# Second stage of a four-layer graph network: another layout of the score rows in DRAM, read back in two pieces, and a copy instead of an addition

## The chip, the cores and the metric

The kernel runs on one core of one Trainium2 chip. The metric is the device time of one execution in microseconds (us); lower is better. A core has a matrix engine (PE), a vector engine (DVE), an activation engine (ACT), a general engine (POOL), a sequencer that here issues the DMAs (SP), and 16 DMA engines that they all share. Each engine works through its own queue in order.

## The reference

Four graph layers run one after the other on x, 128 batches of 128 nodes with 128 features, with one adjacency matrix for each batch. Each layer takes the layer norm of x with relu, computes its update, and adds it to x. The change lies in the second layer, whose score between nodes i and j comes from the absolute difference of their features:

```python
D = jnp.abs(x[:, :, None, :] - x[:, None, :, :])
h = jnp.einsum('bijc,oc->bijo', D, W1) + b1
m = jnp.mean(h, axis=(0, 1, 2))
v = jnp.mean((h - m) ** 2, axis=(0, 1, 2))
h = (h - m) / jnp.sqrt(v + EPS) * g1 + be1
h = _leaky(h)
s = jnp.einsum('bijo,uo->biju', h, W2)[..., 0] + b2[0]
s = jnp.where(A_init > 0, s, NEG)
A = jax.nn.softmax(s, axis=-1)
y = jnp.einsum('bij,bjc->bic', A, x)
```

After that y goes through a linear map, a second batch norm and a third linear map. The scores are symmetric: s(i, j) = s(j, i). Because m and v are taken over all batches, no score can be formed before h is known for all of them.

## The kernel before

The program has three stages. The **first stage** computes layer one, and for layer two the linear values hp of every pair of nodes together with their mean and variance. Thanks to the symmetry only the pairs (i, i + k mod 128) with k from 0 to 64 are needed. The values go out to DRAM as tiles HP, 2 MB for a batch[...].

The **second stage** is `two_stages` from line 770 on. It fetches the values again (`fetch`, L662: two reads of 1 MB for a batch into tiles z, into a ring of 10 buffers), normalises and activates them on ACT and DVE (L850, L854, L868), and PE turns them into scores (`products`, L825). The order of the instructions is written out by hand: `slot(b)` is one step of a software pipeline and handles one batch at each of its places, and `at(slot, place, work)` hangs extra work on a place of a slot: "am", "e", "p", "a", "l", "s" in order of the slot. `slot` copies the scores of the batch before to SBUF (su, L846), PE puts them in order of k (`by_k`, L832), and DVE writes them to a tile sk (`to_sk`, L839 and L841): for each of the 128 nodes i and each of the G = 4 batches of a group, a row of 65 scores, k = 0 to 64, with the first and last halved.

What the softmax needs is a square: node i in a partition, node j along the row. The row of i has to be moved to the right by i places, another distance in each partition[...]. So `chain(turn)`, which handles one group of four batches, sends the rows through DRAM:

- `to_rows` (L902), at place "s" of slot 4 x turn + 5: one DMA writes the 65 scores of row i to DRAM, starting at place i of a row that is ROW = 192 long (128 + 64). Row i starts at 192 i, its scores at 193 i; that is the step `ROW + 1`. The other places were set to zero once (`no_scores`, L579) and stay zero. The DMA right behind it (L905) loads the group's x.
- `from_rows` (L909), two slots later: one DMA reads the four squares of 128 x 192 back into a tile u. It can be issued only when the write has landed, and SP waits for that.
- `folded` (L920), at place "l" of slot s0 = 4 x turn + 9, on DVE: columns 128 to 191 of u are added to columns 0 to 63. These are the scores that had run over the end of the row.
- `turned("put", ...)` (L894) at place "p" of the next slot: PE transposes u, which by symmetry gives the other half of the square. `scores` (L924, L925) on DVE adds the two and masks with `cap`.
- The softmax and the products with the features follow in the next slots, and at slot s0 + 7 the results go out (L957, L958): x1 as x, and y.

There are two DRAM buffers `slots` that take turns, and two buffers of u. POOL has two operations for a group in this stage: x1 = x + bt (L916) and cap (L914), in `normed` at place "e" of slot s0. Between slots 12 and 38 the stage has extra work of `brief`, mostly on DVE (L1045), which prepares and decides for stage three. `final` marks the last group.

The **third stage** computes layers three and four; the change doesn't touch it.

Of the kernel before, what the change touches and what calls it, by code (L numbers as in the profile page):

```python
# [9 lines left out]
F32 = mybir.dt.float32  # L10
# [4 lines left out]
OP = mybir.AluOpType  # L15
AX = mybir.AxisListType

P = 128
G = 4
# [7 lines left out]

KH = 32
KC = 8
ROW = P + 2 * KH  # L30
ON_POOL = {1, 3}
BY_MAX = 0
FETCHED = 10
# [136 lines left out]
def tile_gnn_stack(ctx: ExitStack, tc: tile.TileContext, a: dict, out: bass.AP):  # L170
    nc = tc.nc
# [48 lines left out]

    slots = [dr.tile([G, P, ROW], F32, tag=f"rows{n}", name=f"rows{n}") for n in range(2)]
    AGG = [dr.tile([P, G, P], F32, tag=f"a{g}", name=f"a{g}") for g in range(NG)]
# [44 lines left out]
    def two_stages(general):  # L267
# [6 lines left out]
        with tc.tile_pool(name="c0", bufs=1) as c0, tc.tile_pool(name="p0", bufs=2) as p0:  # L274
# [278 lines left out]
            found = {}  # L553
            zero = c0.tile([P, ROW], F32, name="zero")
            nc.gpsimd.memset(zero, 0.0)
# [21 lines left out]
            def no_scores():  # L577
                for r in slots:
                    nc.sync.dma_start(r.rearrange("g i r -> i g r"), zero[:, None, :].to_broadcast([P, G, ROW]))  # L579

# [191 lines left out]
        with tc.tile_pool(name="c1", bufs=1, reuse_waits="tile") as c1, \  # L772
# [28 lines left out]
            for n in range(2):  # L801
                t = c1.tile([P, G, 1 + 2 * KH], F32, name=f"sk{n}")
# [76 lines left out]
            def chain(turn):  # L879

                rows, own_sk = slots[turn % 2], sk[turn % 2]
                t = {}
                g = (turn - 1) % NG
                final = turn == NG - 1
# [15 lines left out]
                def to_rows():  # L900
                    to = rows[0, 0, 0:1]
                    nc.sync.dma_start(bass.AP(tensor=to.tensor, offset=to.offset,  # L902
                                              ap=[[ROW + 1, P], [P * ROW, G], [1, 1 + 2 * KH]]), own_sk)
                    t["x"] = p1.tile([P, G, P], F32, name="x", bufs=3)
                    nc.sync.dma_start(t["x"], X[g])  # L905

                def from_rows():
                    t["u"] = p1.tile([P, G, ROW], F32, name="u")
                    nc.sync.dma_start(t["u"], rows.rearrange("g i r -> i g r"))  # L909

                def normed():
                    t["h"] = pre_norm(p1, t["x"], MV1[:, g], RS1[:, g])
# [3 lines left out]
                    nc.gpsimd.tensor_tensor(t["x1"], t["x"], over_group(bt), OP.add)  # L916

                def folded():
                    u = t["u"]
                    nc.vector.tensor_tensor(u[:, :, 0:2 * KH], u[:, :, 0:2 * KH], u[:, :, P:], OP.add)  # L920

                def scores():
                    t["e"] = p1.tile([P, G, P], F32, name="e1")
# [30 lines left out]
                def stored():  # L954
                    nc.vector.bn_stats(ST2[:, g, :], t["y"].rearrange("p a b -> p (a b)"))
                    if g not in Y:
                        nc.sync.dma_start(X[g], t["x1"])  # L957
                        nc.sync.dma_start(Z[g], t["y"])  # L958

                at(G * turn + G + 1 - final, "s", to_rows)  # L960
                at(G * turn + G + 3 - 2 * final, "s", from_rows)
                at(s0, "e", normed)
                at(s0, "p", lambda: turned("pt", t["h"]))
                at(s0, "l", folded)
                at(s0 + 1, "am", lambda: copied("hT", "pt"))
                at(s0 + 1, "p", lambda: turned("put", t["u"]))
# [667 lines left out]
```

## Time and profile before

| | us |
|---|---|
| median of 3 runs | 2674.77 (2673.55 to 2675.49) |
| profiled execution, device time | 2676.09 |
| profiled execution, span from first to last instruction | 2674.2 |

Busy shares of the span: PE 91%, DVE 92%, ACT 89%, POOL 64%. They are averages over three stages with different limits. In the second stage, about 1450 to 2245 us, POOL is nearly idle (0 to 1 tenths in the slices) while DVE and PE are busy at 8 to 9 tenths. DMAs of this stage:

| DMA | count | KB each | median us from issue to landing |
|---|---|---|---|
| z <- hp (L662) | 248 | 1024 | 13.7 |
| rows <- sk (L902) | 32 | 130 | 13.0 |
| u <- rows (L909) | 32 | 384 | 11.4 |
| x <- x, all uses | 118 | 256 | 4.8 |
| z <- y (L958) | 27 | 256 | 11.8 |

The profile page shows the span in 40 equal slices of 66.9 us, with the DMA rate in the last row. In a timeline each row has the start, the duration, the engine, the line of the code, the operation, out<-in, the count and in brackets the idle time of the engine just before and what ended it. In a table of waits each row has who waited for whom, us in total, times, and the longest.

### The profile page before, as it was taken

Reading aid. Unit: us, or ns where it says so; the run is one execution under the profiler, and the core shown is the slowest. Engines: PE = TensorE matmul, PEld = TensorE weight load, DVE = VectorE, ACT = ScalarE, POOL = GpSimd, SP = SyncE. Lnnn points to the kernel's source line nnn. Section 1 sums busy time; section 2 is a strip of 40 time slices with the busy share of each in tenths; the row PEclk is TensorE's granted clock in tenths of the full one; section 3 lists DMA queues with packets and bytes.
Section 4 is the critical chain, followed back from the end, with each engine's and each line's share of the span. In section 5 each row is a group of like instructions: output and inputs, shape, how many; then the busy total and the mean of one; then the engine's idle time right before and its main releaser. Section 6 shows DMA issues by size and latency. Waiting matters only on the chain.

```text
span 2674.2 us, 41925 instructions
## 1 busy us (share of the span) xinstructions
PE 2437.0 (91%) x14521; PEld 1162.1 (43%) x14521; DVE 2469.6 (92%) x4738; ACT 2380.3 (89%) x2821; POOL 1706.1 (64%) x1628
## 2 busy tenths in 40 slices
PE   6999999999999999999997988888888886999997
PEld 3333333333333333333332443444444445777776
DVE  5999999999999999999998789988888886899997
ACT  5999999999999999999998877788778874999997
POOL 6999999999999999999985000010101123666663
PEclk8999999999999999999998999999999998999999
DMA  3555555555555555555542999999999992021211
GB/s 101 201 206 209 212 212 211 212 213 205 209 205 209 205 210 204 217 204 216 205 197 93 409 409 384 392 409 410 411 410 411 410 373 81 21 68 56 64 37 34
DMA packets 185426, 611.43 MB, mean 229 GB/s; under 512 B 31987, under 2 KB 99702, under 8 KB 121718
## 3 DMA queue, kind: packets, MB, share of 16 engines
q1 hardware_dynamic: 184768, 608.50, 59.1%
q8 instruction: 118, 1.93, 0.3%
q14 instruction: 102, 0.84, 0.1%
q10 hardware_dynamic: 438, 0.17, 0.0%
HBM read 312.58 MB, written 296.03 MB: 228 GB/s over the span
## 4 chain that ended last, share of the span: by engine, by line
PE 37%; ACT 24%; DVE 15%; DMA 12%; POOL 7%; issue 4%; SPq 0%; POOLq 0%; DVEq 0%; ACTq 0%
PE hp L338 16%; ACT d L376 9%; ACT z L352 7%; DMA z<-hp 4%; PE hp L341 4%; DMA rows<-sk 4%; PE ps L825 4%; POOL d L328 4%; DMA u<-rows 3%; DVE z L868 3%; ACT o L473 2%; PE pk L832 2%; ACT hn L473 2%; PE xp L414 1%; DVE e L1502 1%
## 5 line engine op out<-in xcount | busy, mean ns | idle before, releaser
L328 POOL TENSOR_TENSOR d<-xe 128x2048 f32<-128x2048 f32 x256 | 1073.8, 4205 | 36.4 <-PE hp L338 34.5
L338 PE MATMUL hp<-d,w1T 128*64 128x512 f32 x4096 | 994.1, 601 | 57.6 <-ACT z L352 54.5
L376 ACT ACTIVATE d<-d 128x2048 f32<-128x2048 f32 x384 | 733.8, 1924 | 19.8 <-POOL d L328 19.5
L328 DVE TENSOR_TENSOR d<-xe,xp 128x2048 f32<-128x2048 f32 x256 | 583.6, 2280 | 7.0 <-POOL xe L423 4.0
L352 ACT COPY z<-hp 128x1024 f32<-128x1024 f32 x512 | 519.1, 1015 | 9.7 <-PE hp L338 4.5
L338 PEld LDWEIGHTS hp<-d,w1T 128*64 128x64 f32 x4096 | 276.9, 136 | 559.5 <-issue 455.3
L916 POOL TENSOR_TENSOR x<-x,bt 128x512 f32<-128x512 f32 x32 | 48.8, 1525 | 665.7 <-DMA x<-x 494.1
L366 DVE BATCH_NORM_STATS2 st<-z 128x6 f32<-128x512 f32 x512 | 354.7, 693 | 6.2 <-ACT z L352 6.1
L367 DVE BATCH_NORM_STATS2 st<-z 128x6 f32<-128x512 f32 (+1 forms) x512 | 336.4, 657 | 0.0
L868 DVE SCALAR_TENSOR_TENSOR z<-z 128x2048 f32<-128x2048 f32 x128 | 299.5, 2340 | 5.5 <-ACT z L850 5.3
L850 ACT ACTIVATE z<-z,bias,scale 128x2048 f32<-128x2048 f32 x128 | 267.5, 2090 | 8.9 <-DVE bias L762 7.7
L854 ACT ACTIVATE zr<-z,bias,scale 128x2048 f32<-128x2048 f32 x128 | 267.7, 2092 | 0.5 <-DMA z<-hp 0.5
L341 PE MATMUL hp<-both_t,xw 128*64 128x512 f32 x1024 | 265.2, 592 | 0.0
L825 PE MATMUL ps<-z,w2z 128*32 128x512 f32 x1024 | 140.9, 622 | 61.2 <-DVE z L868 60.5
L832 PEld LDWEIGHTS pk<-pick,su 128*128 128x128 f32 x1024 | 126.8, 195 | 147.8 <-DVE su L846 112.9
L832 PE MATMUL pk<-pick,su 128*128 128x16 f32 x1024 | 139.4, 268 | 34.6 <-DVE su L846 33.8
L825 PE MATMUL ps<-zr,w2r 128*32 128x512 f32 x1024 | 142.5, 629 | 0.0
L341 PEld LDWEIGHTS hp<-both_t,xw 128*64 128x64 f32 x1024 | 77.6, 137 | 142.2 <-issue 142.2
L825 PE MATMUL ps<-z,w2l 128*32 128x512 f32 x1024 | 138.4, 610 | 0.0
L1525 PE MATMUL pv<-wr,e 128*128 128x128 f32 x1024 | 134.0, 278 | 2.1 <-ACT wr L1450 1.1
L1525 PEld LDWEIGHTS pv<-wr,e 128*128 128x128 f32 x1024 | 124.1, 192 | 8.4 <-ACT wr L1450 1.8
L1409 ACT ACTIVATE h<-x,nb,rs 128x128 f32<-128x128 f32 x256 | 106.0, 491 | 20.1 <-POOL nb L1404 18.4
(241 smaller groups left out, 3808.3 us busy)
## 6 DMA issues: line engine op xcount, KB each, us to landing
hp<-z SPq DMA_DIRECT2D x248, 1024.0 KB, 4.0
z<-hp SPq DMA_DIRECT2D x248, 1024.0 KB, 13.7
x<-x SPq DMA_DIRECT2D x118, 256.0 KB, 4.8
u<-rows SPq DMA_DIRECT2D x32, 384.0 KB, 11.4
x<-in_x_dram SPq DMA_DIRECT2D x32, 256.0 KB, 5.6
adj<-in_adj_dram SPq DMA_DIRECT2D x32, 256.0 KB, 5.9
out_dram<-x SPq DMA_DIRECT2D x32, 256.0 KB, 2.4
z<-y SPq DMA_DIRECT2D x27, 256.0 KB, 11.8
```

The lines of the kernel that those rows point to most:

```text
L328: eng.tensor_tensor(d, ahead, x[:, None, None, :].to_broadcast([P, 2, KC, P]), OP.max if t == BY_MAX else OP.subtract)
L338: nc.tensor.matmul(hp[64 * hh:64 * hh + 64, c:c + 512], w1T2 if by_max else w1T, d[:, hh, c:c + 512], start=True, stop=not by_max, skip_gr ...
L341: nc.tensor.matmul(hp[64 * hh:64 * hh + 64, c:c + 512], XW[i // NT // 2][:, i // NT % 2, :], both_t.rearrange("p h k i -> p h (k i)")[:, h ...
L352: nc.scalar.copy(half_of(b, t), linear.pop(i))
L366: nc.vector.bn_stats(st[:, 2 * t, :], hs[:, 0:512])
L367: nc.vector.bn_stats(st[:, 2 * t + 1, :], hs[:, 512:1024 - P * last])
L376: nc.scalar.activation(diffs[i], diffs[i], AF.Abs)
L825: nc.tensor.matmul(ps[32 * c:32 * c + 32, :], w[:, w0:w0 + 32], v[:, 512 * c:512 * c + 512], start=j0 == 0, stop=w is w2r, skip_group_chec ...
L832: nc.tensor.matmul(pk[:, kk, 0:16], su[:, kk, :], pick.rearrange("p h j -> p (h j)"), start=True, stop=True)
L850: nc.scalar.activation(z0, z0, AF.Identity, bias=bias1, scale=scale1[:, 0:1])
L854: nc.scalar.activation(zr, z1, AF.Relu, bias=bias1, scale=scale1[:, 0:1])
L868: nc.vector.scalar_tensor_tensor(z0, z0, 0.01, z0, op0=OP.mult, op1=OP.max)
```

## The change

The rows in DRAM become 129 long, and the scores of row i are written straight, from the start of row i (step `ROW`). Read back with a step of 128 and not 129, row i begins i places earlier relative to its scores, so they appear moved to the right by i: an element at 128 i + c is place c - i of row i. This works while the 65 scores end before column 128, that is for i up to 63. The nodes from 64 on are read with their own start, 64 columns further on: into columns 64 to 191 of u. So `from_rows` has two DMAs, each for 64 partitions and 128 columns. Places that were never written are zero, as before.

In the upper half of u the columns 128 to 191 hold what had run over the end, and columns 0 to 63 hold nothing, so `folded` is a copy there and nothing at all in the lower half: 64 partitions, 4 x 64 elements. It runs on POOL, except in the last group, where it stays on DVE.

```diff
-ROW = P + 2 * KH
+ROW = P + 1
...
                 def to_rows():
                     to = rows[0, 0, 0:1]
                     nc.sync.dma_start(bass.AP(tensor=to.tensor, offset=to.offset,
-                                              ap=[[ROW + 1, P], [P * ROW, G], [1, 1 + 2 * KH]]), own_sk)
+                                              ap=[[ROW, P], [P * ROW, G], [1, 1 + 2 * KH]]), own_sk)
...
                 def from_rows():
-                    t["u"] = p1.tile([P, G, ROW], F32, name="u")
-                    nc.sync.dma_start(t["u"], rows.rearrange("g i r -> i g r"))
+                    t["u"] = p1.tile([P, G, P + 2 * KH], F32, name="u")
+                    for half in range(2):
+                        i = slice(P // 2 * half, P // 2 * half + P // 2)
+                        of = rows[0, 0, 0:1]
+                        of = bass.AP(tensor=of.tensor, offset=of.offset + (P + 1) * P // 2 * half,
+                                     ap=[[P, P // 2], [P * ROW, G], [1, P]])
+                        nc.sync.dma_start(t["u"][i, :, P // 2 * half:P // 2 * half + P], of)
...
                 def folded():
-                    u = t["u"]
-                    nc.vector.tensor_tensor(u[:, :, 0:2 * KH], u[:, :, 0:2 * KH], u[:, :, P:], OP.add)
+                    u = t["u"][P // 2:]
+                    eng = nc.vector if final else nc.gpsimd
+                    eng.tensor_copy(u[:, :, 0:2 * KH], u[:, :, P:])
```

Here P is 128, KH 32 and G 4. The tile of zeros that fills the DRAM rows at the start is [P, ROW] and shrinks with ROW.

## The prediction

> **What bounds the kernel now.** I read the page's 40 slices first. The change touches only the second stage, which is the part in which the DMA engines are full.
>
> ```profile
> DMA  3555555555555555555542999999999992021211
> GB/s 101 201 206 209 212 212 211 212 213 205 209 205 209 205 210 204 217 204 216 205 197 93 409 409 384 392 409 410 411 410 411 410 373 81 21 68 56 64 37 34
> ```
>
> A slice is 66.9 us. From 1471 us (slice 23) the core moves about 410 GB/s for eleven slices, and the figure hardly changes. To see whether that is a ceiling or just what the engines ask for, I cut the stage into stretches (columns: length, busy us and instructions of PE, PEld, DVE, ACT, POOL, PE clock, DMA share, GB/s).
>
> ```profile
> 1480.00:1492.00 12.00, 11.88 (x104) 4.95 (x100) 9.98 (x14) 12.00 (x7) 0.00 (x0) 1.00 1.02 421
> 1648.00:1660.00 12.00, 10.61 (x73) 4.71 (x73) 11.86 (x20) 7.88 (x6) 0.00 (x0) 0.86 1.00 379
> 1804.00:1816.00 12.00, 11.58 (x90) 5.85 (x88) 9.47 (x14) 10.60 (x9) 0.50 (x1) 1.00 1.03 408
> 1710.12:1849.10 138.98, 123.73 (x966) 59.93 (x966) 123.12 (x188) 114.96 (x80) 18.72 (x12) 1.00 1.02 408
> 1934.14:2172.13 237.99, 206.52 (x1580) 99.36 (x1580) 201.91 (x311) 188.41 (x131) 33.87 (x20) 0.99 1.03 410
> ```
>
> Between 1582 and 1710 us DVE has the extra work of `brief` and the DMA rate falls below 380. Everywhere else it is 408 to 410, whether the engines run fast (1710 to 1849) or stall (1934 to 2172). I read that as a ceiling for this mix of transfers; 421 is the highest seen. Next the DMA issues of one late group (four batches) on SP.
>
> ```profile
> 1920.81 0.37 SPq L902 DMA_DIRECT2D rows<-sk  x1
> 1921.91 0.32 SPq L905 DMA_DIRECT2D x<-x  x1
> 1922.60 7.68 SPq L662 DMA_DIRECT2D z<-hp  x4
> 1934.14 0.37 SPq L909 DMA_DIRECT2D u<-rows  x1
> 1934.56 0.50 SPq L957 DMA_DIRECT2D x<-x  x1
> 1935.11 0.42 SPq L958 DMA_DIRECT2D z<-y  x1
> 1935.64 6.82 SPq L662 DMA_DIRECT2D z<-hp  x4
> ...
> 2172.13 0.37 SPq L909 DMA_DIRECT2D u<-rows  x1
> ```
>
> The u reads at 1934.14 and 2172.13 are ten groups apart, so one group takes 23.80 us. By the sizes in the page's DMA issues it moves 8 x 1024 (z) + 3 x 256 (x in, x and y out) + 384 (u) + 130 (rows) = 9474 KB = 9.70 MB, hence 408 GB/s: the group's length is its bytes. The rows need 13.3 us to land, u another 11.7, both queued behind z rows. That is where the engines feel the DMA:
>
> ```profile
> 1943.30 0.15 DVE L841 TENSOR_SCALAR sk<-sk 128x1 f32<-128x1 f32 x1
> 1945.84 0.43 DVE L920 TENSOR_TENSOR u<-u 128x256 f32<-128x256 f32 x1 [2.39 <-DMA u<-rows]
> 1946.19 0.69 DVE L846 COPY su<-ps 128x512 f32<-128x512 f32 x1
> ...
> 1949.88 0.60 PE L894 MATMUL pt<-ident,u 128*128 128x128 f32 x4
> ...
> DVE u L920 <- DMA u<-rows: 30.0, 17, 5.7
> ```
>
> The fold L920 waits at the head of DVE's queue (30.0 us in 17 groups) with su and then PE behind it; PE does not need the folded u until 1949.88.
>
> [...] No row of this trace has a large transfer to 64 partitions; the nearest is u<-rows on all 128, which shares the 408. [...] POOL's cap (L914) takes 0.62 us or, beside DVE, 2.54 and 2.55; so I give the copy on POOL 0.4 to 2.6 us (it has half of cap's elements per partition).
>
> **The change, part by part.**
>
> *Bytes of the read.* u shrinks from 512 pieces of 768 B to 512 of 512 B: 128 KB less, 0.131 MB / 409 GB/s = 0.32 us a group. It counts where the DMA is the limit: 4 groups from 1486 to 1582 us and (2182.73 - 1710.12) / 23.6 = 20 from 1710 to the last rows write under load. 24 x 0.32 = 7.7 us less. Cheap end: the whole mix could run at the 421 seen once; then a group is 9.57 / 421 = 22.7 us, 1.1 less. Dear end: [...] the old read costs 0.393 / 409 = 0.96: 0.32 more a group, +7.7. I take the byte price[...].
>
> *The write of rows* keeps its 512 pieces of 260 B; only their step changes, 772 to 516 B. Nothing. The zero fill at 27 us (2 x 384 KB, no one waits for it) gets smaller, and the memset before it (0.26 us on POOL) too: nothing.
>
> *The second DMA issue.* SP issues one more DMA a group, 0.37 us; the x and y stores and the next z reads move back by that. SP waits 213.6 us in 180 waits of L662 for PE to free z, so it is hidden; without that cover it would be 0.4 us x 32 = 13 us. Both halves wait for the rows, which SP already waits for (L909, 84.3 us in 27 waits); the second adds no wait if it isn't ordered behind the first.
>
> *The fold leaves DVE.* DVE loses 0.45 us a group (14.3 us over 32) and the 30.0 us of waits. In the DMA-bound groups this can't shorten the group: the stall moves on. In the five groups of `brief`, DVE is busy 11.86 of 12 us in the full stretches, and 5 x 0.43 = 2.1 us come free[...]. I take -1 us.
>
> *The wait moves from DVE to POOL.* Behind it on POOL stand cap (0.6 to 2.6 us) and x1 (1.3 to 3.2) of the next group, needed a group later: free. Who waits for POOL is PE's transposes of u. In the group above u is wanted at 1949.88 and landed at 1945.8: 4.1 us for a copy of 0.4 to 2.6. So u may come some 2 to 4 us later than now before anything stalls, and the engines may get about 2 us further ahead of the DMA queue. The bytes arrive no sooner, but when the last z lands (about 2200 us) 2 us less remain to do: -2 us, once. Next late thing is that PE transpose.
>
> *The last turn* keeps its copy on DVE, at most the 0.40 us that the fold takes, and its two short reads land in about the old 3.3 us: nothing.
>
> Sum: -7.7 - 1 - 2 = -10.7 us. The profiled execution took 2676.1 us (span 2674.2 and 1.9 around it), 1.3 above the median 2674.8; against that median the sum is 2664, and I say 2665.
>
> **Rivals.**
> 1. [...] (no net change in DMA time): the loss of the halves eats the saved bytes, and -3 remains: 2672. [...] Against: the deep queue.
> 2. [...] the case on the other side[...]. +7.7 - 2 = +6: 2681. It decides once the two halves cost over 1.28 us a group, 0.3 more than now. For it: the flat 408, which leaves no slack to hide a slower read. [...]
> 3. *The stall was the limit, not the bytes*: with DVE unblocked the DMA goes to 421, 20 groups x 1.1 = 21, with 3 more: about 2651. Against: the same 408 with and without stalls.
> 4. *The second half is ordered behind the first* (both write tile u): SP then stands 11 us a group before the z reads and u lands 11 us later, of which slack covers 5: some 6 us x 24, over 2750. Against: they touch disjoint partitions, and the three loads into one small tile at 0.7, 1.3 and 1.5 us weren't held apart.
>
> **How the numbers follow.** Forecast 0.40, rivals 0.21, 0.28, 0.05 and 0.06. About 0.2% (5.3 us) is what can be told from no change. The forecast case is faster nearly always (0.37), rival 1 mostly the same (0.15), rival 2 split (0.17 slower, 0.11 same), 3 faster, 4 slower: faster 0.46, same 0.29, slower 0.25. The forecast case by itself spans 2658 to 2671; 2652 to 2686 takes in rivals 1 and 2 and leaves out most of 3 and 4.
>
> **What would show it.** Right: late groups at 23.5 us with the rate still about 408; no DVE wait for u; POOL copies of 0.4 to 2.6 us; rows and u landing 1 to 2 us later than now. Wrong: groups at 24 us with a rate under 405[...]; PE waiting at the transposes of u by as much as DVE did; the two u reads on SP more than 1 us apart; a rate well above 410.

## The result and the profile after

| | before | after |
|---|---|---|
| median of 6 runs each, us | 2674.95 (2673.39 to 2679.0) | 2695.16 (2693.8 to 2702.1) |
| ratio, 95% interval | | 1.0079 [1.0066, 1.0092] |
| profiled execution, span, us | 2674.2 | 2693.2 |

The change makes the kernel 20 us slower, where 10 us faster was forecast. 2695 lies outside the stated range, 2652 to 2686, too.

The page of the changed kernel first: the DMA rows of the 40 slices (67.3 us each), the two lines of the chain of waits, and the reads of u among the DMA issues.

```profile
DMA  3555555555555555555553999999999993021211
GB/s 100 198 212 212 212 206 207 206 214 206 215 203 212 206 215 204 207 204 210 214 206 115 385 395 392 392 382 388 391 383 391 381 380 92 21 68 56 64 36 34
...
PE 33%; DMA 22%; ACT 21%; DVE 11%; POOL 8%; issue 5%; SPq 0%; POOLq 0%; ACTq 0%; DVEq 0%
PE hp L338 16%; DMA u<-rows 11%; DMA rows<-sk 11%; ACT z L352 7%; ACT d L376 7%; PE hp L341 4%; POOL d L328 3%; ACT o L473 2%; DVE z L868 2%; ACT hn L473 2%; PE pv L1535 1%; PE xp L414 1%; PE ps L825 1%; DVE e L1512 1%; PE ph L491 1%
...
u<-rows SPq DMA_DIRECT2D x64, 128.0 KB, 12.3
```

The DMA engines are as full as before (9 in every slice of the stage), but they move 380 to 395 GB/s instead of some 410. The chain now runs through the two small transfers of the ring, the write of rows and the read of u: 11% of the span each.

The same stretches of the stage in the changed kernel (columns as in the prediction: length, busy us and instructions of PE, PEld, DVE, ACT, POOL, PE clock, DMA share, GB/s):

```profile
1480.00:1580.00 100.00, 86.89 (x653) 39.18 (x645) 81.58 (x138) 77.91 (x52) 13.94 (x13) 0.93 1.03 391
1580.00:1710.00 130.00, 110.66 (x823) 53.74 (x826) 121.49 (x196) 96.69 (x67) 18.22 (x15) 0.96 1.03 391
1710.00:1850.00 140.00, 118.80 (x904) 55.74 (x900) 111.20 (x169) 107.27 (x77) 15.45 (x17) 0.99 1.02 387
1934.14:2172.13 237.99, 204.55 (x1504) 95.95 (x1503) 186.48 (x285) 177.44 (x124) 23.67 (x30) 0.96 1.02 387
```

From 1934 to 2172 the rate is 387 where it was 410, at the same DMA share. So the engines don't stand idle; what they move takes them longer. DVE has 15 us less to do there. The ten folds that have left it are 10 x 0.43 = 4 us of that; the rest is work that arrives later (285 instructions instead of 311).

The DMA issues of one late group on SP, with two other reads of u:

```profile
1724.05 1.24 SPq L918 DMA_DIRECT2D u<-rows  x2
...
1911.08 0.37 SPq L902 DMA_DIRECT2D rows<-sk  x1
...
1923.14 1.24 SPq L918 DMA_DIRECT2D u<-rows  x2
1924.43 0.60 SPq L967 DMA_DIRECT2D x<-x  x1
1925.13 0.38 SPq L968 DMA_DIRECT2D z<-y  x1
1926.13 8.90 SPq L662 DMA_DIRECT2D z<-hp  x4
1935.56 0.37 SPq L902 DMA_DIRECT2D rows<-sk  x1
...
2196.08 1.24 SPq L918 DMA_DIRECT2D u<-rows  x2
```

Both halves are issued within 1.24 us, so SP doesn't hold the second behind the first. From the read at 1724.05 to the one at 2196.08 are 19 groups: 24.84 us a group. The same two reads of the kernel before, the tenth and the 29th of its 32, stand at 1720.83 and 2172.13: 23.75 us. These two reads cut every run of this study into three parts, and the table in the next section is made of them.

Last, what had been the stall at the head of DVE's queue: the copy, PE's transposes and the addition behind it in one group, and the waits from 1480 to 2240 us.

```profile
1936.14 0.40 POOL L930 COPY u<-u 64x256 f32<-64x256 f32 x1 [10.50 <-DMA u<-rows]
1936.59 0.66 PE L894 MATMUL pt<-ident,u 128*128 128x128 f32 x4 [1.62 <-POOL u L930]
1937.34 0.69 DVE L934 TENSOR_TENSOR e<-u,pt 128x512 f32<-128x512 f32 x1 [3.91 <-PE pt L894]
```

```profile
POOL u L930 <- DMA u<-rows: 309.2, 29, 11.7
...
DVE e L934 <- PE pt L894: 106.4, 30, 5.6
...
PEld pt L894 <- POOL u L930: 64.8, 26, 3.8
PE pt L894 <- POOL u L930: 43.5, 23, 2.9
```

The copy takes 0.40 us (median of 31, at most 2.47), as forecast, and its wait of 309 us costs POOL nothing. But PE now waits for u in nearly every group (26 and 23 waits in the last two rows) and DVE waits for PE behind it: 3.91 us here, 106.4 us in 30 waits, where it was 50.8 us in 32 in the kernel before. There PE wanted the folded u 4 us after it had landed.

### The profile page after: what moved, and what is told of

The parts are those of the page before. It is cut to its first block, busy times and chain, and to the rows that moved or that the text cites. A ratio compares the mean times of both kernels' runs of the same rounds, so it can differ in the third digit from the quotient of the medians.

```text
span 2693.2 us, 42077 instructions
## 1 busy us (share of the span) xinstructions
PE 2443.8 (91%) x14521; PEld 1159.1 (43%) x14521; DVE 2450.3 (91%) x4707; ACT 2377.6 (88%) x2821; POOL 1710.5 (64%) x1659
## 4 chain that ended last, share of the span: by engine, by line
PE 33%; DMA 22%; ACT 21%; DVE 11%; POOL 8%; issue 5%; SPq 0%; POOLq 0%; ACTq 0%; DVEq 0%
PE hp L338 16%; DMA u<-rows 11%; DMA rows<-sk 11%; ACT z L352 7%; ACT d L376 7%; PE hp L341 4%; POOL d L328 3%; ACT o L473 2%; DVE z L868 2%; ACT hn L473 2%; PE pv L1535 1%; PE xp L414 1%; PE ps L825 1%; DVE e L1512 1%; PE ph L491 1%
## 5 line engine op out<-in xcount | busy, mean ns | idle before, releaser
L366 DVE BATCH_NORM_STATS2 st<-z 128x6 f32<-128x512 f32 x512 | 348.5, 681 | 6.1 <-ACT z L352 6.0
L367 DVE BATCH_NORM_STATS2 st<-z 128x6 f32<-128x512 f32 (+1 forms) x512 | 330.0, 644 | 0.0
L868 DVE SCALAR_TENSOR_TENSOR z<-z 128x2048 f32<-128x2048 f32 x128 | 293.1, 2290 | 11.4 <-ACT z L850 11.3
L930 POOL COPY u<-u 64x256 f32<-64x256 f32 x31 | 19.0, 611 | 320.6 <-DMA u<-rows 309.2
```

Source lines behind the costliest of these rows:

```text
L366: nc.vector.bn_stats(st[:, 2 * t, :], hs[:, 0:512])
L367: nc.vector.bn_stats(st[:, 2 * t + 1, :], hs[:, 512:1024 - P * last])
L868: nc.vector.scalar_tensor_tensor(z0, z0, 0.01, z0, op0=OP.mult, op1=OP.max)
```

## The experiments

Two theories stood at the start. *Ports* (the name of a guess; no trace shows a port): 64 partitions next to each other are a slow target, wherever the bytes come from. *Order*: the second DMA itself, the eight DMA completion semaphores of the program, or the rows' new layout in DRAM hold the ring up. The chain of waits speaks for the second one:

```profile
1911.08 11.99 DMA rows<-sk
...
1923.14 12.36 DMA u<-rows
...
1935.56 12.00 DMA rows<-sk
```

These are pieces of the changed kernel's chain in order of time: the ring (the write of rows and the read of u, group after group) does nothing but wait for its own two transfers. The write of rows at 1935.56 needs nothing from u. It is the eighth DMA after the first half of u (u, u, x, y, four z, rows). In the trace SP's DMAs take turns at eight completion semaphores, the write has the same one as the half issued at 1923.14, and SP waits for u ahead of the write of rows 26 times, each time until the read has landed (12.0 us in all). With one read of u the eighth before it would be another DMA.

In all experiments the three parts of the span are measured at the tenth and the 29th read of u (us, from the one profiled execution of each kernel; those of e1, e3 and e7 were 5.5 to 7.1 us below their medians):

| kernel | read of u: KB, to which partitions | fold or copy | to the 10th read | a group, over 19 | from the 29th read to the end | median |
|---|---|---|---|---|---|---|
| before | 384, all | DVE | 1720.8 | 23.75 | 502.1 | 2674.95 |
| e2 | 2 x 192, all | DVE | 1718.5 | 23.74 | 501.8 | 2672.88 |
| e6 | 2 x 192, even, odd | DVE | 1719.5 | 23.78 | 502.1 | 2674.1 |
| e3 | 2 x 192, lower, upper | DVE | 1729.6 | 26.02 | 504.0 | 2735.4 |
| e4 | 384, all | POOL | 1714.3 | 23.76 | 496.1 | 2663.3 |
| e8, as e4 | 384, all | POOL | 1715.7 | 23.74 | 497.8 | 2666.4 |
| e11 | 256, all | DVE | 1717.3 | 23.46 | 503.8 | 2668.38 |
| e1 | 256, all | POOL | 1715.3 | 23.41 | 496.0 | 2663.64 |
| e7 | 2 x 128, even, odd | POOL | 1712.3 | 23.44 | 495.6 | 2662.31 |
| e9 | 2 x 128, even, odd | POOL | 1714.2 | 23.45 | 494.4 | 2657.87 |
| e10 | 2 x 128, lower, upper | POOL | 1723.3 | 24.99 | 496.8 | 2695.4 |
| e5 | 2 x 128, lower, upper | DVE | 1723.8 | 25.00 | 503.8 | 2701.86 |
| after | 2 x 128, lower, upper | POOL | 1724.1 | 24.84 | 497.1 | 2695.16 |

The kernel before measured 2674.37, 2674.28 and 2673.03 beside e1 to e4, e5 to e8 and e9 to e11.

### e1: one read of 256 KB

The change with one read of all partitions, 128 columns each. The scores of nodes 64 to 127 are read from the same start as the others, so they stand 64 columns off.

```diff
-                    for half in range(2):
-                        i = slice(P // 2 * half, P // 2 * half + P // 2)
-                        of = rows[0, 0, 0:1]
-                        of = bass.AP(tensor=of.tensor, offset=of.offset + (P + 1) * P // 2 * half,
-                                     ap=[[P, P // 2], [P * ROW, G], [1, P]])
-                        nc.sync.dma_start(t["u"][i, :, P // 2 * half:P // 2 * half + P], of)
+                    of = rows[0, 0, 0:1]
+                    of = bass.AP(tensor=of.tensor, offset=of.offset, ap=[[P, P], [P * ROW, G], [1, P]])
+                    nc.sync.dma_start(t["u"][:, :, 0:P], of)
...
-                    eng.tensor_copy(u[:, :, 0:2 * KH], u[:, :, P:])
+                    eng.tensor_copy(u[:, :, 0:2 * KH], u[:, :, 2 * KH:P])
```

> The changed kernel with one read of all 128 partitions and 128 columns (step 128) in place of the two halves, so 13 DMAs a group again and 256 KB; the scores of nodes 64 to 127 are left unshifted, so their part of the softmax is not the reference's. Ports[...]: the loss goes and the saved bytes come through, about 2665 us. Count (the fourteenth DMA of a group delays the others): also about 2665. Write (rows 516 B apart are slow to write): stays near 2695.

2663.64 us, ratio 0.9959 [0.9945, 0.9973]. Bytes and POOL alone make the kernel 11 us faster, close to the forecast sum of -10.7. So the loss sits in the two halves: in their number or in their shape.

### e2 and e3: the kernel before, its read in two

Nothing else of the change. e2 splits the 384 KB by batches, each part on all partitions; e3 into lower and upper partitions.

```diff
-                    nc.sync.dma_start(t["u"], rows.rearrange("g i r -> i g r"))
+                    for k in (0, 2):
+                        nc.sync.dma_start(t["u"][:, k:k + 2, :], rows[k:k + 2].rearrange("g i r -> i g r"))
```

```diff
-                    nc.sync.dma_start(t["u"], rows.rearrange("g i r -> i g r"))
+                    for i in (slice(0, P // 2), slice(P // 2, P)):
+                        nc.sync.dma_start(t["u"][i], rows[:, i, :].rearrange("g i r -> i g r"))
```

> The kernel before with its read of u in two DMAs of 128 partitions, two batches each: 14 DMAs a group[...]. Ports: 2675, as before. Count: about 2695, as the changed kernel. Write: 2675.

> The kernel before with its read of u in two DMAs of 64 partitions, all 192 columns each: 14 DMAs a group[...]. Ports: [...] at least 1 us a group and with the 26 groups under load 2700 to 2715. Count: 2695, the same as with the split by batch. Write: 2675.

e2: 2672.88, ratio 0.9995 [0.9986, 1.0004], no difference. e3: 2735.4, ratio 1.0233 [1.0209, 1.0257], 61 us slower than before with the same bytes, the same count of DMAs as e2 and none of the change's other parts. That is 20 us beyond the upper end of the expected 2700 to 2715, for which 1 us a group was the author's estimate; by the table it is 26.02 - 23.75 = 2.27 us.

### e4 and e8: the fold on POOL

The kernel before with the addition on POOL in all groups but the last; e8 is the same kernel, measured again.

```diff
-                    nc.vector.tensor_tensor(u[:, :, 0:2 * KH], u[:, :, 0:2 * KH], u[:, :, P:], OP.add)
+                    eng = nc.vector if final else nc.gpsimd
+                    eng.tensor_tensor(u[:, :, 0:2 * KH], u[:, :, 0:2 * KH], u[:, :, P:], OP.add)
```

> The kernel before with its addition L920 on POOL except in the last group, nothing else. If the engines are only held by the DMA: 2670 to 2675, a few us at most. If the move to POOL is a part of the loss: over 2680.

> The kernel before with only its addition L920 on POOL except in the last group, in more rounds. Measured once at 0.9961 of before. If the saved bytes are worth anything beyond the move to POOL, the changed kernel by parity (256 KB, POOL) must lie below this one by up to 8 us; if not, both at 2664.

2663.3 and 2666.4, ratios 0.9961 [0.9949, 0.9973] and 0.9966 [0.9953, 0.9978]: 8 to 11 us faster than before, and 29 to 32 faster than the change. That is below both of the times expected for e4, and this version beats both kernels. In the table e4's gain is 6.5 us ahead of the tenth read and 6.0 behind the 29th (e8: 5.1 and 4.3), and nothing in the 19 groups between, which stay at 23.76 us. Two windows of e4 (columns as above):

```profile
1580.00:1710.00 130.00, 111.05 (x829) 53.29 (x827) 121.48 (x195) 96.69 (x68) 22.14 (x17) 0.96 1.02 406
1850.00:2150.00 300.00, 262.75 (x2032) 125.18 (x2024) 253.62 (x388) 240.55 (x167) 39.96 (x37) 0.99 1.03 410
```

The same two of the kernel before:

```profile
1580.00:1710.00 130.00, 109.46 (x807) 51.80 (x800) 121.20 (x198) 96.53 (x67) 10.67 (x10) 0.95 1.01 389
1850.00:2150.00 300.00, 264.82 (x2008) 126.91 (x2007) 254.75 (x392) 238.33 (x165) 37.42 (x25) 0.98 1.03 410
```

With the addition on POOL the DMA runs at 406 instead of 389 where `brief` loads DVE (the prediction reads this stretch as below 380). It would be natural to put that down to the fold's wait in DVE's queue, but in this stretch the kernel before has no such wait. The line L920 from 1580 to 1710 us, with nothing listed under either heading:

```profile
L920 DVE TENSOR_TENSOR u<-u x5: 414/416/418, 1583.9 to 1689.7; 128x256 f32<-128x256 f32 x5
its engine sat idle before it (us, times) until:
who waited for it (us, times):
```

DVE is busy for 121 of the 130 us in both kernels. What leaves it is 5 x 0.42 = 2.1 us, 1.6% of the stretch, while the rate rises by 4.4%; where the rest comes from isn't shown. The other pairs rise less: 398 in e1 against 388 in e11, 391 in the change against 382 in e5. In the late groups the rate stays at 410: there the stall, 18.8 of its 30.0 us between 1850 and 2150, wasn't the limit.

### e5: the copy on DVE

```diff
-                    eng = nc.vector if final else nc.gpsimd
+                    eng = nc.vector
```

> The changed kernel with its copy of u on DVE in every group, not only in the last. Before plus this is the change without POOL. Ports: the reads cost what they cost and POOL saves some 11 us, as it did in the kernel before, so about 2706 us. If the copy on POOL is what hurts the changed kernel: 2675 or less.

2701.86, ratio 1.0095 [1.008, 1.0109]: 6.7 us more than the change. POOL still helps there, and it isn't what makes the change slow. By the table most of the difference is in the part behind the 29th read, 503.8 against 497.1; the 19 groups between show 3.0 us of it, the part ahead of them none.

### e6 and e7: even and odd partitions

e6 is e3 with other partitions, two reads of 192 KB to every second one. e7 is the change with reads for every second node, to every second partition; as in e1, nodes 64 to 127 are read 64 columns off.

```diff
-                    nc.sync.dma_start(t["u"], rows.rearrange("g i r -> i g r"))
+                    for i in (slice(0, P, 2), slice(1, P, 2)):
+                        nc.sync.dma_start(t["u"][i], rows[:, i, :].rearrange("g i r -> i g r"))
```

```diff
-                        i = slice(P // 2 * half, P // 2 * half + P // 2)
...
-                        of = bass.AP(tensor=of.tensor, offset=of.offset + (P + 1) * P // 2 * half,
-                                     ap=[[P, P // 2], [P * ROW, G], [1, P]])
-                        nc.sync.dma_start(t["u"][i, :, P // 2 * half:P // 2 * half + P], of)
+                        of = bass.AP(tensor=of.tensor, offset=of.offset + P * half,
+                                     ap=[[2 * P, P // 2], [P * ROW, G], [1, P]])
+                        nc.sync.dma_start(t["u"][half::2, :, 0:P], of)
...
-                    eng.tensor_copy(u[:, :, 0:2 * KH], u[:, :, P:])
+                    eng.tensor_copy(u[:, :, 0:2 * KH], u[:, :, 2 * KH:P])
```

> The kernel before with its read of u in two DMAs of 64 partitions, the even and then the odd ones, all 192 columns: 14 DMAs a group of 64 partitions each, but each spread over the whole range of partitions. Ports: the same as one read, 2675. If it is the count of partitions in a DMA that costs (how a DMA is dealt out to the engines): 2735, as with the split in lower and upper half.

> The changed kernel with its two reads taking the even and the odd partitions in place of the lower and the upper ones, 64 partitions and 128 columns each, all else as in the change; the scores of nodes 64 to 127 are left unshifted. Ports: about 2664, as with one read of all partitions. If two reads of 64 partitions cost by themselves: 2695.

e6: 2674.1, ratio 1.0 [0.9993, 1.0006]. e7: 2662.31, ratio 0.9949 [0.9935, 0.9963]. Each read still fills 64 partitions and each group still issues 14 DMAs, but nothing is lost. What e7 leaves open is that it also reads other rows of DRAM in each DMA.

### e9 and e10: source and target crossed

e9 reads the change's own halves of DRAM into even and odd partitions. e10 reads e7's every second row into lower and upper partitions. In both the rows of u stand in another order than the nodes (in e10 nodes 64 to 127 are 64 columns off as well).

```diff
-                        nc.sync.dma_start(t["u"][i, :, P // 2 * half:P // 2 * half + P], of)
+                        nc.sync.dma_start(t["u"][half::2, :, 0:P], of)
...
-                    eng.tensor_copy(u[:, :, 0:2 * KH], u[:, :, P:])
+                    eng.tensor_copy(u[:, :, 0:2 * KH], u[:, :, 2 * KH:P])
```

e10 is e7 with this:

```diff
-                        nc.sync.dma_start(t["u"][half::2, :, 0:P], of)
+                        i = slice(P // 2 * half, P // 2 * half + P // 2)
+                        nc.sync.dma_start(t["u"][i, :, 0:P], of)
```

> The changed kernel reading exactly the DRAM rows of its two halves, but writing the first half to the even and the second to the odd partitions of u; the rows of u are then in another order, so the scores are not the reference's. If the loss comes from where in SBUF the reads land: about 2662, as with parity on both sides. If it comes from which DRAM rows a read takes: 2695.

> The converse: even and odd rows in DRAM, written to the lower and to the upper 64 partitions of u; again the order of rows in u is another one and the scores are not the reference's. Landing place: 2695. DRAM rows: about 2662.

e9: 2657.87, ratio 0.9946 [0.9929, 0.9963]. e10: 2695.4, ratio 1.0081 [1.0066, 1.0097], the time of the change. The rows in DRAM make no difference clear of the noise; the partitions decide, by 37.5 us between e10 and e9 and by 33.1 between e10 and e7. The lines of the chain on the page of e9:

```profile
PE 42%; ACT 22%; DVE 18%; POOL 7%; issue 6%; DMA 5%; SPq 0%; DVEq 0%; POOLq 0%; ACTq 0%
PE hp L338 17%; ACT d L376 8%; ACT z L352 8%; PE ps L825 6%; DVE z L868 5%; PE hp L341 4%; POOL d L328 3%; DMA rows<-sk 3%; PE pk L832 2%; ACT o L473 2%; PE pv L1535 2%; DMA u<-rows 2%; ACT hn L473 2%; PE xp L414 1%; PE ph L491 1%
```

The same 14 DMAs a group with the same waits, and the ring has 5% of the chain instead of 22%. The chain of the changed kernel names who waits; it does not name why the transfers take 12 us each.

The DMA view counts packets by size, and in this stage the sizes from 512 B to 2 KB are the 512 pieces of u alone. So the difference of two of its counts shows where a read of u passes. For the change, the stretches that begin 2.4, 3.6, 4.8 and 10.8 us after the issue at 1923.14, 1.2 us each:

```profile
DMA packets 168, 0.46 MB, mean 380 GB/s; under 512 B 13, under 2 KB 119, under 8 KB 119
DMA packets 214, 0.30 MB, mean 251 GB/s; under 512 B 16, under 2 KB 160, under 8 KB 195
DMA packets 262, 0.42 MB, mean 349 GB/s; under 512 B 23, under 2 KB 157, under 8 KB 240
...
DMA packets 99, 0.45 MB, mean 377 GB/s; under 512 B 13, under 2 KB 45, under 8 KB 46
```

For e9, beginning 6.0, 7.2, 8.4 and 9.6 us after the issue at 1924.45:

```profile
DMA packets 166, 0.48 MB, mean 404 GB/s; under 512 B 15, under 2 KB 109, under 8 KB 114
DMA packets 236, 0.47 MB, mean 395 GB/s; under 512 B 19, under 2 KB 149, under 8 KB 200
DMA packets 274, 0.43 MB, mean 362 GB/s; under 512 B 22, under 2 KB 183, under 8 KB 247
DMA packets 266, 0.50 MB, mean 416 GB/s; under 512 B 23, under 2 KB 150, under 8 KB 234
```

Pieces of u in such stretches, from the same counts in four kernels (each row adds up to 512):

| begins, us after the issue | 2.4 | 3.6 | 4.8 | 6.0 | 7.2 | 8.4 | 9.6 | 10.8 | 12.0 |
|---|---|---|---|---|---|---|---|---|---|
| before | 0 | 0 | 23 | 123 | 113 | 125 | 108 | 20 | 0 |
| e9 | 0 | 0 | 0 | 94 | 130 | 161 | 127 | 0 | 0 |
| after | 106 | 144 | 134 | 73 | 23 | 0 | 0 | 32 | 0 |
| e10 | 130 | 111 | 112 | 64 | 31 | 29 | 3 | 28 | 4 |

Two things are seen. The rate falls while the pieces of the halves pass, to 251 GB/s in the worst stretch (226 in the worst 0.61 us), while e9 never falls below 362. From 2.4 to 8.4 us the change loses (30 + 159 + 61 + 41 + 55) x 1.2 / 410 = 1.0 us against a steady 410 (the other two stretches were at 369 and 355). And most pieces of the halves pass early, within 7 us of the issue, but the last 32 come at 11 to 12 us, and only then has u landed. So it is in each of the 20 groups from the tenth to the 29th read: the first of the last 32 pieces starts 1.5 to 5.5 us behind the 480th, in e9 at most 0.13 us. 32 is 512 / 16, what one of the 16 engines would have if the pieces were dealt evenly; which engine lags, and why, these views don't show. (Early pieces alone are nothing special: in the 29th group of the kernel before and of e9 the first ones also pass some 3 us after the issue.)

Whose pieces take longer? The trace keeps the start, the size and the time of every DMA piece. Here they are added up from the tenth to the 29th read and divided by 16 engines and 19 groups, in us, with the mean time of one piece in brackets. Pieces of z have 8192 B, those of x and y 2048 B; the rest are the write of rows and pieces of 4 B.

| kernel | u | z | x and y | rest | sum | a group |
|---|---|---|---|---|---|---|
| e9 | 0.87 (27.2 ns) | 20.19 (315.0 ns) | 2.16 (90.1 ns) | 0.74 | 23.96 | 23.45 |
| after | 1.20 (37.5 ns) | 21.16 (329.7 ns) | 2.26 (94.4 ns) | 0.75 | 25.37 | 24.84 |
| e6 | 1.19 (37.1 ns) | 20.22 (314.9 ns) | 2.14 (89.4 ns) | 0.74 | 24.29 | 23.78 |
| e3 | 1.75 (54.6 ns) | 21.74 (338.1 ns) | 2.28 (95.2 ns) | 0.76 | 26.53 | 26.02 |

The longer pieces account for the whole loss: 1.41 us between the change and e9, whose groups differ by 1.39, and 2.24 us between e3 and e6, whose groups differ by 2.24 (in all four kernels the sum is 2% above the group, as the DMA share of 1.02 says). But only a quarter of it is in u itself. About 0.97 of the 1.41 us is in z. In the change a piece of z during which pieces of u start takes 365 ns on average and any other 322; in e9 these are 314 and 315.

### e11: 256 KB, the copy on DVE

e1 with `eng = nc.vector` in every group; nodes 64 to 127 stand 64 columns off as there.

> One read of all 128 partitions and 128 columns (256 KB, step 128), with the copy on DVE in every group: the saved bytes without POOL and without the halves; the scores of nodes 64 to 127 are left unshifted. If the bytes alone set the length of a group: 0.32 us less in 24 groups, about 2666. If the groups are held by what DVE waits for and not by bytes: 2672 to 2676.

2668.38, ratio 0.9983 [0.9974, 0.9991]: the bytes alone bring 4.6 us, and a group shrinks by 0.29 us. The time lies between the two that were expected, nearer to that of the bytes. With the operation on POOL the same bytes show less in the medians: e1 and e4 are level (2663.64 and 2663.3), and e7 is 4 us below e8.

## Why the prediction was wrong

**The step that failed** is the price of the read: "I take the byte price". That price counts the read by itself, and what is measured lies mostly beside it: the z rows that pass beside the halves take longer themselves, 365 ns a piece against 322 for the other z rows. On 256 KB the halves cost 24.84 - 23.45 = 1.39 us a group more than e9's even and odd partitions, and in the table of pieces 0.97 us of that loss is in z, 0.33 in u and 0.10 in x and y. Charged to the read alone, on top of its byte price of 0.262 MB / 410 GB/s = 0.64 us, that makes 2.03 us, as if its bytes had moved at 129 GB/s. In the kernel before, e3 against e6, it is 26.02 - 23.78 = 2.24 us on 384 KB (z 1.52, u 0.56, x and y 0.14), so the loss grows with the bytes. The prediction's own first sign of being wrong, groups at 24 us with a rate under 405, is what came: 24.84 us and 387 to 391 GB/s.

**The dear end was too cheap as well.** Rival 2 had the right sign, but its 1.28 us a group, 0.32 more than the old read, was the author's estimate; nothing measured before the change showed the price of a read into 64 partitions. The halves' own pieces did take 1.20 us of the 16 engines; what the estimate has no term for is z, and with z the halves cost 2.03. Against the old read of 0.96 us that is 1.07 more, not 0.32; the table's 24.84 - 23.75 = 1.09 agrees. Over 19 groups this is 20.7 us; ahead of the tenth read the change is 3.2 us later and behind the 29th 5.0 us shorter, in sum the 19.0 us between the two spans.

The halves' own pieces go at 0.73 of the rate of e9's, 37.5 ns against 27.2. What slows them isn't shown; the runs show that the partitions decide, 2695.4 us in e10 against 2657.87 in e9.

**The bytes** were right where they were counted, in the groups: -0.29 us a group where -0.32 was forecast. In the medians they gave -4.6 us (e11) where -7.7 was, and on top of POOL 0 to 4.

**The fold leaving DVE and the wait moving to POOL** were forecast at -1 (the author's estimate, about half of the 2.1 us that leave DVE) and -2 us; e4 and e8 show -8 to -11. The places were the right ones, `brief` and the end, but both were mis-sized. Ahead of the tenth read the gain is 6.5 us in e4 and 5.1 in e8, but 2.0 from e11 to e1 and none from e5 to the change, so the move alone doesn't set it; only the 2.1 us of DVE's own time are seen to go, and the excess stays unexplained. At the end it is 6.0 and 4.3 us in e4 and e8, 7.8 from e11 to e1 and 6.7 from e5 to the change. More than half of each falls before the last read of u, which comes 50.1 us behind the 29th in the kernel before and 46.7 in e4 and e8. Why the end gains so much and not 2 wasn't tried.

**The second DMA issue** at nothing was right: e2 and e6 are at 0.9995 and 1.0. Rival 4 fell with the 1.24 us for both halves. Rival 3 fell with e4: no stall at L920 and still 410 GB/s. Rival 1, a loss that just eats the saved bytes, was too mild by the same term as rival 2.

Without the failed step the sum stood: -10.7 us forecast, -10.7 (e1), -12.0 (e7) and -15.2 (e9) measured. That it came so close is luck: the bytes gave less and POOL more than their terms.

**Open**: why the halves and the pieces beside them slow down, and which engine lags. The ring's wait for the eighth DMA before it adds nothing that shows: the longer pieces account for the whole of the longer group, and e6, e7 and e9 issue the same 14 DMAs in the same order at no cost. Other blocks of 64 neighbouring partitions, and one half without the other, weren't tried. A version with the bytes of the change and the scores of all nodes in their places, on even and odd partitions, would need nodes in another order throughout and wasn't tried.

## What to carry to other kernels

Before a transfer is split, look at which partitions each part fills: parts on all partitions or on every second one cost nothing here (e2 and e6, ratios 0.9995 and 1.0), while lower and upper halves of the same bytes cost 33 to 61 us, with most of the longer DMA time in the transfers beside them. When a chain of waits names a DMA, compare the rate and the packets in the same stretch with a kernel that has the same waits; only then is it clear whether the order or the transfer is at fault. An operation at the head of a busy engine's queue can be worth moving to an idle engine even where the DMA is the bound for most of the stage: 7 to 11 us here, most of it outside the groups that the DMA bounds.

## What was not expected of the hardware

- Two small reads, one into the lower and one into the upper 64 partitions, cost more in the transfers beside them than in themselves: of 1.41 us of longer DMA time a group 0.97 is in z. Charged to the reads alone it is as if they moved at 129 GB/s in a queue that otherwise moves 410. Two reads into the even and the odd partitions cost nothing (e6, ratio 1.0).
- A small transfer lands with its last pieces, and these can be far behind the others: 480 of the 512 pieces had passed 8.4 us after the issue, and the last 32 came between 10.8 and 12.0 us. The mean rate of that last stretch, 377 GB/s, doesn't show it.
